# Two graph layers with layernorm: normalization on ScalarE, the adjacency scaled in its own period, two relus behind the next bank copy

## Chip, cores, metric

The kernel runs on one core of a Trainium2 chip. The metric is the device time of one execution in microseconds; a lower one is better. Runs of the kernel before agreed within 0.3% on every chip used.

## The reference, cut to what matters

There are 128 graphs of 128 nodes with 512 features, all fp32.

```python
# layer 0
deg = sum(adj, -1);  agg = (adj @ x) / max(deg, 1e-6)
x = layernorm(x + relu(concat(x, agg) @ W.T))
# layer 1
h = relu(adj @ (x @ W1) + b1)
h = relu(adj @ (h @ W2) + b2)
x = layernorm(x + adj @ (h @ W3) + b3)
# layernorm(v) = (v - mean) / sqrt(var + 1e-5), over the 512 features
```

## The kernel before

Four graphs make a period, and there are 32 periods. A period runs layer 0 and the start of layer 1 for its own graphs (`y`, `l`, `g`, `h1`) mixed with the rest of layer 1 for the graphs of the period before (`s2`, `h2`, `s3`, `o`), so that TensorE always has something to do. Each large product is made of seven smaller ones on 2x2 blocks. Three banks of PSUM (`py`, `pz`, `px`) hold them; a bank is copied to SBUF by ScalarE in the middle of the work, and **TensorE may add to that bank again only when the copy is done** (in the kernel before, the second y_y group waits for y_s in 30 periods, 108.2 us in all).

```python
def wino_a(key, a, b, c00, c11, transposed=False, inner=None):
    py, pz, px = bank(f"{key}_y"), bank(f"{key}_z"), bank(f"{key}_x")
    product(py, a, b, 1, True, transposed)
    s1 = copied(py, f"{key}_s1")            # ScalarE
    product(pz, a, b, 5, True, transposed)
    product(py, a, b, 6, False, transposed) # adds to py: waits for s1
    s2 = copied(py, f"{key}_s2")
    product(px, a, b, 2, True, transposed)
    ...
    product(py, a, b, 7, False, transposed) # waits for s2
```

The blocks that go with it (GpSimd, four instructions) are made by `data_blocks`; only those of the input x are pinned, which keeps an instruction behind all that was written before it on its engine. What isn't pinned is ordered at build time by the framework's scheduler, which may let an instruction overtake another that it takes to be not ready yet. The engines then keep that order: in the kernel before, a y_s copy whose data are there at 1025.4 starts at 1030.01, behind two relus.

```python
def data_blocks(t, name, pin=False):
    a00, a01 = t[:, 0:2, 0:2, :], t[:, 2:4, 0:2, :]
    a10, a11 = t[:, 0:2, 2:4, :], t[:, 2:4, 2:4, :]
    ...
    for dst, a, b, op in ((s1, a10, a11, OP.add), (s2, s1, a00, OP.subtract),
                          (a10, a00, a10, OP.subtract), (s4, a01, s2, OP.subtract)):
        ins = add(dst, a, b, op, nc.gpsimd)
        if pin:
            pinned(ins)

def layernorm(t, gs, name, store=None):
    ...                                     # VectorE: statistics; GpSimd: rstd
    for i, g in enumerate(gs):
        nc.vector.tensor_scalar(
            t[:, g, :], t[:, g, :], mv[:, i, 0:1], rstd[:, 1, i : i + 1], op0=OP.subtract, op1=OP.mult)

def sums_cols(q, m, n):                     # h1: add on VectorE, then relu on ScalarE
    def f(s, p):
        add(cols(H1[q], m, n), ...)
        ...
        if (m, n) == (0, 1):                # the last add
            relu_cols(q, 2, 0, 2)
            relu_cols(q, 3, 0, 2)
    return f

for t in range(NG + 1):
    ...
    if new: seg_h1_a(t)
    if old: seg_last(t - 1, (2, 3))         # o: add, layernorm, store
    if more:
        XA[t + 1] = data_blocks(XT[t + 1], f"x_{t + 1}", pin=True)
        normalized(t + 1)                   # ah = at * r on VectorE
    if new: seg_h1_b(t)                     # last add and relus of h1; then the h blocks on GpSimd
```

## Time and profile before

| | before |
|---|---|
| time, median | 2587.95 us (2587.63 to 2588.99) |
| TensorE busy | 2443.3 us, 94% |
| VectorE, ScalarE, GpSimd busy | 38%, 23%, 36% |
| longest wait of TensorE | y_y for ScalarE's copy y_s: 108.2 us in 30 times |
| mean granted clock of TensorE | 0.975 |

A row of the waits reads: who waited, for whom, us in total, times, longest. A line of the timeline reads: start, duration, engine, source line, operation, output <- input, count, and in brackets the idle time before it and what ended it. Many instructions have the line of a helper (L77 is every add), so they are told apart by their tiles: `u` and `o` are the rows that the layernorm of layer 0 and of layer 1 works on, `rstd` is 1 / sqrt(var + eps), `ah` the scaled adjacency. A name with _s is ScalarE's copy of a bank (`y_s` of `y_y`) or, on a POOL (GpSimd) line, a block sum for a product (`x_s`, `h_s`). A product has four matmuls in the program and eight in the profile. A product's group on TensorE is listed with 1.89 us, and the next one starts 1.73 us after it (in the kernel before, y_y at 1023.49 and y_z at 1025.22); for the pace one subtracts starts. The granted clock is TensorE's clock as the profiler recorded it, 1 being full speed.

### The profile page before, as it was taken

The numbers are of one execution on the slowest core, as the hardware profiler recorded it, in microseconds if no ns is written. First come the engines' busy times: TensorE is split into PE (matmuls) and PEld (weight loads), VectorE is DVE, ScalarE is ACT, GpSimd is POOL, SyncE is SP. The second block draws the span as 40 slices with busy tenths as digits, with TensorE's granted clock in tenths as the row PEclk, the third lists the DMA queues.
The fourth block names the chain that finished last, engine by engine and source line by source line (L and its number), as shares of the span: only waits on it lengthen the run. The fifth ranks groups of instructions, "written<-read, shape, count | busy, mean of one in ns | idle before, by whom it ended". The sixth has DMA issues, their size and how long they took to land.

```text
span 2585.6 us, 29247 instructions
## 1 busy us (share of the span) xinstructions
PE 2443.3 (94%) x11776; PEld 2110.4 (82%) x11776; DVE 988.5 (38%) x1685; ACT 594.9 (23%) x1025; POOL 942.9 (36%) x900
## 2 busy tenths in 40 slices
PE   6999999999999999999999999999999999999997
PEld 5888888888888888888888888888888888888886
DVE  4334433334433344333443333443334433344333
ACT  1222222222222222222222222222222222222221
POOL 1343423334333343233442343423334333344233
PEclk8999999999999999999999999999999999999999
DMA  4111101111101111011110111111112111111100
GB/s 171 46 45 62 62 29 50 46 61 62 48 32 60 46 61 62 29 49 45 62 62 29 49 45 62 62 36 42 62 45 62 57 33 49 46 62 61 29 9 33
DMA packets 53125, 133.28 MB, mean 52 GB/s; under 512 B 21632, under 2 KB 21632, under 8 KB 44800
## 3 DMA queue, kind: packets, MB, share of 16 engines
q1 hardware_dynamic: 52992, 131.42, 15.2%
q8 instruction: 94, 1.54, 0.3%
q14 instruction: 39, 0.32, 0.1%
HBM read 97.78 MB, written 33.62 MB: 51 GB/s over the span
## 4 chain that ended last, share of the span: by engine, by line
PE 81%; DVE 9%; issue 4%; ACT 3%; POOL 2%; DMA 1%; SPq 0%; POOLq 0%; DVEq 0%; ACTq 0%
PE s_y L187 17%; PE s_z L187 9%; PE l_y L187 8%; PE y_y L187 8%; PE g L304 5%; PE h L357 4%; PE s_x L187 4%; PE h_y L187 4%; PE y_x L187 2%; PE h_z L187 2%; PE y_z L187 2%; PE l_v L187 2%; PE h_x L187 2%; PE l_x L187 2%; PE l_z L187 2%
## 5 line engine op out<-in xcount | busy, mean ns | idle before, releaser
L77 POOL TENSOR_TENSOR h_s<-h 128x512 f32<-128x512 f32 x64 | 81.1, 1267 | 873.3 <-ACT h L358 837.6
L176 ACT COPY s_s<-s_y 128x512 f32<-128x512 f32 x192 | 112.4, 585 | 627.3 <-PE s_y L187 538.4
L187 PE MATMUL s_z<-w,h_s 128*128 128x256 f32 x1024 | 242.9, 380 | 2.9 <-POOL h_s L77 2.9
L187 PE MATMUL s_y<-w_t,h 128*128 128x256 f32 x1024 | 242.1, 379 | 0.7 <-ACT s_s L176 0.7
L187 PEld LDWEIGHTS s_z<-w,h_s 128*128 128x128 f32 x1024 | 194.8, 190 | 30.2 <-POOL h_s L77 3.7
L187 PEld LDWEIGHTS s_y<-w_t,h 128*128 128x128 f32 x1024 | 192.0, 190 | 25.8 <-ACT s_s L176 1.1
L187 PE MATMUL y_y<-wb_t,x_s 128*128 128x256 f32 x256 | 96.3, 542 | 108.2 <-ACT y_s L176 108.2
L77 DVE TENSOR_TENSOR s<-s_z,s_s 128x512 f32<-128x512 f32 x128 | 88.5, 692 | 258.6 <-PE s_z L187 183.4
L254 POOL TENSOR_SCALAR rstd<-mv 128x2 f32<-128x2 f32 x128 | 27.9, 218 | 437.2 <-DVE mv L252 437.2
L187 PEld LDWEIGHTS y_y<-wb_t,x_s 128*128 128x128 f32 x256 | 68.1, 278 | 132.5 <-issue 119.3
L257 DVE TENSOR_SCALAR o<-o,mv,rstd 128x512 f32<-128x512 f32 x128 | 120.8, 984 | 127.8 <-POOL rstd L255 127.8
L77 POOL TENSOR_TENSOR u<-u,b 128x512 f32<-128x512 f32 x128 | 158.2, 1267 | 0.0
L77 POOL TENSOR_TENSOR g_s<-g 128x512 f32<-128x512 f32 x32 | 40.6, 1270 | 298.3 <-ACT g L305 298.3
L304 PEld LDWEIGHTS g<-at,u 128*128 128x128 f32 x1024 | 126.7, 195 | 8.8 <-DVE u L257 5.7
L304 PE MATMUL g<-at,u 128*128 128x128 f32 x1024 | 127.1, 278 | 5.3 <-DVE u L257 5.3
L315 ACT ACTIVATE h<-h,b 128x512 f32<-128x512 f32 (+1 forms) x128 | 71.7, 607 | 246.8 <-DVE h L77 246.8
L176 ACT COPY l_s<-l_y 128x512 f32<-128x512 f32 x96 | 56.2, 585 | 310.0 <-PE l_y L187 310.0
L187 PE MATMUL l_y<-wa_t,xT 128*128 128x256 f32 x512 | 122.5, 383 | 0.0
L187 PE MATMUL s_y<-w_t,h_s 128*128 128x256 f32 x512 | 121.8, 381 | 0.0
L187 PE MATMUL h_z<-g_s,w 128*128 128x256 f32 x512 | 121.0, 379 | 0.3 <-POOL g_s L77 0.3
L187 PE MATMUL y_z<-wb,x_s 128*128 128x256 f32 x512 | 121.2, 380 | 0.0
L357 PEld LDWEIGHTS h<-at,s 128*128 128x128 f32 x1024 | 119.6, 192 | 1.8
(97 smaller groups left out, 4716.5 us busy)
## 6 DMA issues: line engine op xcount, KB each, us to landing
xT<-in_xT_dram SPq DMA_DIRECT2D x32, 1024.0 KB, 6.2
x<-in_x_dram SPq DMA_DIRECT2D x32, 1024.0 KB, 4.8
out_dram<-o SPq DMA_DIRECT2D x64, 512.0 KB, 3.0
ar<-in_adj_dram SPq DMA_DIRECT2D x32, 256.0 KB, 6.4
at<-in_adjT_dram SPq DMA_DIRECT2D x32, 256.0 KB, 6.2
r<-dd SPq DMA_DIRECT2D x32, 256.0 KB, 4.7
w<-in_w_dram SPq DMA_DIRECT2D x3, 1024.0 KB, 12.3
wb<-in_w0T_dram SPq DMA_DIRECT2D x1, 1024.0 KB, 5.6
```

What stands on the lines that cost most here:

```text
L77: return (engine or nc.vector).tensor_tensor(dst, a, b, op=op)
L176: nc.scalar.copy(t, p)
L187: nc.tensor.matmul(p[:, o, :], lhsT, rhs, start=start and o == 0 and c == 0, stop=c == 1, skip_group_check=True)
L254: nc.gpsimd.tensor_scalar(rstd[:, 0, :], mv[:, :, 1], LN_EPS, None, op0=OP.add)
L257: nc.vector.tensor_scalar(t[:, g, :], t[:, g, :], mv[:, i, 0:1], rstd[:, 1, i : i + 1], op0=OP.subtract, op1=OP.mult)
L304: nc.tensor.matmul(p[:, c, :], U[q][:, g, c * P : (c + 1) * P], AT[q][:, g, :], start=True, stop=True)
L315: nc.scalar.activation(t, t, AF.Relu, bias=b1_sb[:, c : c + 1])
L357: nc.tensor.matmul(p[:, g, :], S2[q][:, g, o * P : (o + 1) * P], AT[q][:, g, :], start=True, stop=True)
```

## The change

Its intent: the chain of VectorE work in front of the y_s copy is to become shorter (normalization goes to the idler ScalarE, the scaling of the adjacency to a quiet place), and the copy is no longer to stand behind relus that wait for that chain.

```diff
     def normalized(q):
-        AH[q] = loads.tile([P, G, P], F32, tag="ah", name=f"ah_{q}")
+        AH[q] = loads.tile([P, G, P], F32, tag="ah", name=f"ah_{q}", bufs=1)
 ...
-    normalized(0)
     w1_sb = weight_blocks(w1_raw, "w1")
 ...
-    def wino_a(key, a, b, c00, c11, transposed=False, inner=None):
+    def wino_a(key, a, b, c00, c11, transposed=False, inner=None, after_s1=None):
 ...
         s1 = copied(py, f"{key}_s1")
+        if after_s1 is not None:
+            after_s1()
 ... layernorm
-        rstd = small.tile([P, 2, k], F32, tag="rstd", name=f"rstd_{name}")
+        rstd = small.tile([P, 3, k], F32, tag="rstd", name=f"rstd_{name}")
         nc.gpsimd.tensor_scalar(rstd[:, 0, :], mv[:, :, 1], LN_EPS, None, op0=OP.add)
         nc.gpsimd.tensor_tensor(rstd[:, 1, :], rstd[:, 0, :], neg_half[:, 0:k], op=OP.pow)
+        nc.gpsimd.tensor_scalar(rstd[:, 0, :], mv[:, :, 0], -1.0, None, op0=OP.mult)
+        nc.gpsimd.tensor_tensor(rstd[:, 2, :], rstd[:, 0, :], rstd[:, 1, :], op=OP.mult)
         for i, g in enumerate(gs):
-            nc.vector.tensor_scalar(
-                t[:, g, :], t[:, g, :], mv[:, i, 0:1], rstd[:, 1, i : i + 1], op0=OP.subtract, op1=OP.mult
+            nc.scalar.activation(
+                t[:, g, :], t[:, g, :], AF.Identity, bias=rstd[:, 2, i : i + 1], scale=rstd[:, 1, i : i + 1]
             )
 ... seg_y_a
-        wino_a(f"y_{q}", XA[q], wb_sb, sums_to(Y[q], 0, 0), sums_to(Y[q], 1, 1))
+        wino_a(
+            f"y_{q}", XA[q], wb_sb, sums_to(Y[q], 0, 0), sums_to(Y[q], 1, 1),
+            after_s1=(lambda: finish_h1(q - 1)) if q >= 1 else None,
+        )
 ... sums_cols
-            if (m, n) == (0, 1):
-                relu_cols(q, 2, 0, 2)
-                relu_cols(q, 3, 0, 2)
+            if (m, n) == (1, 1):
+                relu_cols(q, 2, 1, 2)
+                relu_cols(q, 3, 1, 2)
 ... seg_h1_b
+    def finish_h1(q):
+        pinned(relu_cols(q, 2, 0, 1))
+        pinned(relu_cols(q, 3, 0, 1))
         HA[q] = data_blocks(H1[q], f"h1_{q}")
 ... the loop
         if new:
             seg_y_a(t)
+        else:
+            finish_h1(t - 1)
 ...
             seg_y_b(t)
+            normalized(t)
 ...
             XA[t + 1] = data_blocks(XT[t + 1], f"x_{t + 1}", pin=True)
-            normalized(t + 1)
```

Below, part 1 is the normalization, part 2 the adjacency scaling, part 3 the relus.

More of the change, by code (lines that the diff above doesn't have):

```diff
@@ L314, in relu_cols @@
         t = H1[q][:, c, 2 * m0 : 2 * m1, :]
-        nc.scalar.activation(t, t, AF.Relu, bias=b1_sb[:, c : c + 1])
+        return nc.scalar.activation(t, t, AF.Relu, bias=b1_sb[:, c : c + 1])
     def sums_cols(q, m, n):
```

## The prediction

> **What bounds the kernel now.** I read the page's engine shares first: TensorE computes for 94% of the span, no other engine for 40%.
>
> ```profile
> PE 2443.3 (94%) x11776; PEld 2110.4 (82%) x11776; DVE 988.5 (38%) x1685; ACT 594.9 (23%) x1025; POOL 942.9 (36%) x900
> ```
>
> So time can only come from TensorE's idle or slow moments. The waits of TensorE name them; one row dwarfs the rest:
>
> ```profile
> PE y_y L187 <- ACT y_s L176: 108.2, 30, 3.6
> PE y_y L187 <- DMA xT<-in_xT_dram: 8.9, 1, 8.9
> PE g L304 <- DVE u L257: 5.3, 1, 5.3
> PE l_x L195 <- DVE ah L146: 5.2, 1, 5.2
> ```
>
> Thirty times, once in nearly every one of 32 periods (a period handles four graphs), TensorE waits 3.6 us for ScalarE's copy y_s of the first bank of the product y. The timeline around one such wait (start us, us, engine, what) shows why a 0.56 us copy comes so late:
>
> ```profile
> 1022.82 0.71 POOL L255 TENSOR_TENSOR rstd<-rstd,neg_half 128x2 f32<-128x2 f32 x1
> ...
> 1023.49 1.89 PE L187 MATMUL y_y<-wb,xT 128*128 128x256 f32 x8
> 1023.50 1.26 POOL L77 TENSOR_TENSOR x_s<-xT 128x512 f32<-128x512 f32 x1
> 1023.57 2.89 DVE L257 TENSOR_SCALAR o<-o,mv,rstd 128x512 f32<-128x512 f32 x2 [1.14 <-POOL rstd L255]
> ...
> 1025.22 1.89 PE L187 MATMUL y_z<-wb,x_s 128*128 128x256 f32 x8
> ...
> 1026.38 1.75 DVE L146 TENSOR_TENSOR ah<-at,r 128x512 f32<-128x512 f32 x1
> ...
> 1028.05 0.68 DVE L77 TENSOR_TENSOR h<-h_z,h_s 128x512 f32<-128x512 f32 x1
> ...
> 1028.77 1.33 ACT L315 ACTIVATE h<-h,b 128x512 f32<-128x512 f32 x2 [5.96 <-DVE h L77]
> 1030.01 0.56 ACT L176 COPY y_s<-y_y 128x512 f32<-128x512 f32 x1
> ...
> 1030.71 3.38 PE L187 MATMUL y_y<-wb_t,x_s 128*128 128x256 f32 x8 [3.61 <-ACT y_s L176]
> 1033.93 1.89 PE L187 MATMUL y_x<-wb,xT 128*128 128x256 f32 x8
> ```
>
> The copy's data are there at about 1025.4, when the first y_y group ends. But on ScalarE it stands behind two relus of h; these need an add on VectorE; that add (its product h_z was done near 1023.65) stands behind two layernorm normalizations of o and the adjacency scaling ah. All of it runs while GpSimd makes the four x_s blocks.
>
> The size of the loss: the second y_y would have begun at 1025.22 + 1.73 = 1026.95 and began at 1030.71: 3.76. It then took 1033.93 - 1030.71 = 3.22 from start to start where eight such matmuls take 1.73: 1.49 more. Together 5.25 us. Check by period: one of the first g groups starts at 1000.94, the same one at 1080.67, so a period is 79.73. Its work back to back is 35 product groups of 1.727, four aggregates of 0.863, h 3.57, g 2 x 1.78 and o 2 x 1.72: 74.5. The difference, 5.2, is this one gap. Times 30: **157 us, 6.1% of the time**. Without it the kernel would take about 2588 - 157 = 2431 us.
>
> [...] 3.76 us idle, then a group at 3.22 for 1.73. Removing the gap also removes the slow group. [...] y_s is ready at 1025.4 and starts at 1030.01. So the order of the instructions on ScalarE decides this change. [...] the two o normalizations take 2.89 here (u's two take 1.01 with GpSimd idle), and ah 1.75 here where in the first period, alone, it took 0.69. [...] The trace has the form with bias alone at 0.71 (L315, 128x512)[...]. [...]
>
> **The change part by part.**
> *Normalization to ScalarE.* Removes from VectorE, per period, four u normalizations (0.54 each) and four o (0.98 mean): 6.1 us. [...] ScalarE's busy time rises from 595 to some 790, 32%: no bound. GpSimd gets two more small instructions per pair (-mean, times rstd). By L254 (0.22) and a gap of 0.08 each that is 0.6 us per pair, 2.4 per period, and it lies **on the path**: each normalization comes 0.6 later.
> *Adjacency scaling.* ah moves to about 1050, behind the last y add, where VectorE is idle for over 2 us. It is needed at 1059.8, and r is there since the period before. It costs nothing there and frees VectorE here. One buffer is enough: its last reader is the aggregate at about 1071.
> *Relus.* Two of the four half-relus (0.45 each) move up behind the add at 1019.14; the other two move behind y_s. So y_s waits no longer for the last h add.
>
> At the old gap, then: h add at about 1023.7 to 1024.4; rstd ready about 1024.15; two o normalizations on ScalarE to about 1025.65; y_s to 1026.25; the second y_y at 1026.95 **without a wait**, 0.7 to spare. The relus follow to 1027.2, GpSimd finishes x_s by about 1029.6 (four at 1.27 to 1.4), the h blocks by 1034.7; the first is needed at about 1033.9 and is ready at 1030.9. The gap goes whole: -157.
>
> New waits[...]:
> (a) The x_s blocks stand behind the 0.6 us of new GpSimd work: the first ends at 1025.4 instead of 1024.76, and y_z's weights are loaded from 1025.0. Wait 0.3 to 0.4.
> (b) In u's layernorm the first rstd is ready at about 1077.5, where the second s_s copy is ready at 1077.4 and the next s_y wants it done by 1078.94. Behind two normalizations it ends at 1079.6 (wait 0.7), behind four at 1081.3 (wait 2.4, unless the scheduler has put the g matmuls first, then 0.6), before them none. Mean by my weights 1.0.
> (c) In o's first layernorm rstd is ready about 1015.6 (GpSimd does the g blocks until 1013.9), and the second h_s copy is ready at 1015.07. If normalizations are ahead of it, it ends at 1017.7 and h_y7, due 1016.59, waits 1.1. I take 0.4 as the mean.
> Sum 1.75 per period, 30 x 1.75 = 53 us. First period and tail: a later last normalization (+1), a tail wait for h_s (2.55) that shortens by about 1: nothing. 2588 - 157 + 53 = 2484; since the scheduler fills holes that it sees with other ready matmuls I lean a little lower: **2474 us**.
>
> **Rivals.** *The wait only changes place:* ScalarE, in order, holds bank copies behind normalizations that wait for GpSimd. For it: the eight new instructions fall among the copies, and rstd took 1.14 us where a scheduler may reckon less. Against it: normalizations are ready within a microsecond or two of the copies, and none sits behind a 6 us chain. If (b) and (c) are at their worst, 2.4 and 1.1 with a dropped clock after one (+1.5): 5.2 per period, and the time stays at 2580. *GpSimd becomes the bound:* 36% busy, +2.4 of 80 us per period: no, but it is the engine of (a). *The gap was hidden anyway:* no; the chain of waits goes through it and the period's sum shows it bare. *All gone, nothing new:* 2431.
>
> **Range and chances.** The floor is 2431; the middle has 1 to 2.5 us of new waits per period (2460 to 2506); a bad order of ScalarE gives 2530 and more. So 2433 to 2534. Faster by over 2% needs under 2536, that is new waits under 3.5 us per period: 0.89. Within 2% 0.10, slower 0.01.
>
> **What would show it.** Right: the row of y_y waiting for y_s is gone; the slow y_y group is back at 1.73; o normalizations no longer appear on VectorE, ah takes 0.69; a period lasts 74.8 to 77; small new rows name y_z waiting for x_s, s_y for s_s, h_y for h_s. Wrong: one of these rows with over 3 us each time, with a slow group behind it.

## The result, and the profile after

| | before | after |
|---|---|---|
| time, median of 4 | 2588.01 us | 2592.41 us |
| VectorE busy | 988.5 us | 779.0 us |
| ScalarE busy | 594.9 us | 792.8 us |
| mean granted clock of TensorE | 0.975 | 0.996 |
| y_y waiting for y_s | 108.2 us | no such row |

The ratio is 1.0016, with a 95% interval of 0.9999 to 1.0034: the time is the same. Ratios here are the mean time of one kernel's fast runs over that of the other's fast runs of the same rounds, so they are not quite the ratio of the medians quoted. The predicted 2474 us, and the range up to 2534, were wrong.

The busy line of the changed kernel's page:

```profile
PE 2423.8 (94%) x11776; PEld 2077.1 (80%) x11776; DVE 779.0 (30%) x1429; ACT 792.8 (31%) x1345; POOL 974.2 (38%) x1156
```

The work moved as planned, and TensorE is as far from full as before. Its waits in the changed kernel:

```profile
PE s_y L186 <- ACT s_s L175: 55.4, 33, 1.7
PE y_z L186 <- POOL x_s L77: 34.0, 30, 1.3
PE h_y L186 <- ACT h_s L175: 31.5, 31, 1.0
PE y_y L186 <- POOL x_s L77: 13.8, 30, 0.5
```

The old wait has gone, and four new rows stand in its place, each once per period: 4.3 us per period by these rows. The timeline of one period shows how each is made; the first five lines belong to s_y, the next three to h_y, the rest to y_z and y_y:

```profile
998.96 1.52 ACT L260 ACTIVATE u<-u,rstd 128x512 f32<-128x512 f32 x2 [2.90 <-POOL rstd L258]
...
1000.45 0.61 PE L310 MATMUL g<-at,u 128*128 128x128 f32 x4
1000.66 1.52 ACT L260 ACTIVATE u<-u,rstd 128x512 f32<-128x512 f32 x2 [0.18 <-POOL rstd L258]
...
1002.09 0.56 ACT L175 COPY s_s<-s_y 128x512 f32<-128x512 f32 x1
1002.79 1.96 PE L186 MATMUL s_y<-w_t,h 128*128 128x256 f32 x8 [1.73 <-ACT s_s L175]
...
1018.84 1.52 ACT L260 ACTIVATE o<-o,rstd 128x512 f32<-128x512 f32 x2 [3.38 <-POOL rstd L258]
...
1020.27 0.56 ACT L175 COPY h_s<-h_y 128x512 f32<-128x512 f32 x1
...
1020.97 1.97 PE L186 MATMUL h_y<-g,w_t 128*128 128x256 f32 x8 [1.01 <-ACT h_s L175]
...
1028.27 1.27 POOL L77 TENSOR_TENSOR h_s<-h 128x512 f32<-128x512 f32 x1
1029.49 0.20 POOL L258 TENSOR_TENSOR rstd<-rstd 128x2 f32<-128x2 f32 x1
1029.64 1.26 POOL L77 TENSOR_TENSOR x_s<-xT 128x512 f32<-128x512 f32 x1
...
1030.86 1.27 POOL L77 TENSOR_TENSOR h_s<-h_s,h 128x512 f32<-128x512 f32 x1
1030.96 1.99 PE L186 MATMUL y_z<-wb,x_s 128*128 128x256 f32 x8 [1.12 <-POOL x_s L77]
1031.15 0.56 ACT L175 COPY y_s<-y_y 128x512 f32<-128x512 f32 x1
...
1032.10 1.26 POOL L77 TENSOR_TENSOR x_s<-x_s,xT 128x512 f32<-128x512 f32 x1
...
1033.41 1.99 PE L186 MATMUL y_y<-wb_t,x_s 128*128 128x256 f32 x8 [0.46 <-POOL x_s L77]
1035.24 1.89 PE L186 MATMUL y_x<-wb,xT 128*128 128x256 f32 x8
```

- **s_y**: the second s_s copy stands behind all four normalizations of u, which end at 1002.2; its data are there at about 998.9 (the group before it starts at 997.00 and is listed with 1.89), and it starts at 1002.09. The scheduler filled part of the hole with four g matmuls (0.44 us). TensorE is idle from 1000.90 to 1002.79, and the group after it takes 0.07 more than 1.73: 1.96 us in all.
- **h_y**: the second h_s copy stands behind the first two normalizations of o. Idle 1.17 us, and the restart 0.07: 1.24.
- **y_z and y_y**: on GpSimd, one of the four h blocks stands ahead of the last small instruction of rstd, and so ahead of the first x_s block; a second one stands between the first and second x_s block. The first x_s block starts at 1029.64, though its input xT was there before: TensorE reads it from 1027.94 on. By starts: y_z begins 1.29 late, y_y follows 0.72 late, and the group after y_y 0.10: 2.11.

The sum is 1.96 + 1.24 + 2.11 = 5.3 us per period, against the 5.25 that the old gap had cost. That the two are so close is a coincidence of sizes: no run links them, and each new wait can be removed alone (below). A period is 79.80 us (s_x at 998.73, the next at 1078.53), where it was 79.73.

### The profile page after: what moved, and what is told of

Its sections match the earlier page's. It is cut to its first block, busy times and chain, and to the rows that moved or that the text cites. A ratio compares the mean times of both kernels' runs of the same rounds, so it can differ in the third digit from the quotient of the medians.

```text
span 2590.0 us, 29418 instructions
## 1 busy us (share of the span) xinstructions
PE 2423.8 (94%) x11776; PEld 2077.1 (80%) x11776; DVE 779.0 (30%) x1429; ACT 792.8 (31%) x1345; POOL 974.2 (38%) x1156
## 4 chain that ended last, share of the span: by engine, by line
PE 63%; POOL 19%; DVE 7%; ACT 6%; issue 4%; DMA 1%; SPq 0%; POOLq 0%; ACTq 0%; DVEq 0%
PE s_y L186 13%; PE l_y L186 8%; PE y_y L186 7%; PE s_z L186 6%; POOL g_s L77 5%; PE h L367 4%; PE g L310 4%; POOL rstd L256 4%; DVE st L252 3%; POOL h_s L77 3%; POOL x_s L77 3%; PE h_y L186 3%; PE s_x L186 2%; PE y_z L186 2%; PE l_v L186 2%
## 5 line engine op out<-in xcount | busy, mean ns | idle before, releaser
L186 PE MATMUL s_y<-w_t,h 128*128 128x256 f32 x1024 | 244.4, 382 | 54.3 <-ACT s_s L175 54.3
L255 POOL TENSOR_SCALAR rstd<-mv 128x2 f32<-128x2 f32 x128 | 28.1, 219 | 416.5 <-DVE mv L253 411.1
L260 ACT ACTIVATE o<-o,rstd 128x512 f32<-128x512 f32 x128 | 97.2, 806 | 190.4 <-POOL rstd L258 190.4
L186 PE MATMUL h_y<-g,w_t 128*128 128x256 f32 x512 | 123.4, 384 | 31.5 <-ACT h_s L175 31.5
L186 PEld LDWEIGHTS h_y<-g,w_t 128*128 128x128 f32 x512 | 94.7, 190 | 68.1 <-issue 57.9
L186 PEld LDWEIGHTS y_z<-wb,x_s 128*128 128x128 f32 x512 | 95.5, 191 | 58.1 <-POOL x_s L77 46.1
L260 ACT ACTIVATE u<-u,rstd 128x512 f32<-128x512 f32 x128 | 97.2, 806 | 106.5 <-POOL rstd L258 106.5
L77 DVE TENSOR_TENSOR s<-s_x,s_s 128x512 f32<-128x512 f32 x64 | 44.3, 692 | 276.9 <-PE s_x L186 276.9
```

The source lines that it names most:

```text
L77: return (engine or nc.vector).tensor_tensor(dst, a, b, op=op)
L186: nc.tensor.matmul(p[:, o, :], lhsT, rhs, start=start and o == 0 and c == 0, stop=c == 1, skip_group_check=True)
L255: nc.gpsimd.tensor_scalar(rstd[:, 0, :], mv[:, :, 1], LN_EPS, None, op0=OP.add)
L260: nc.scalar.activation(t[:, g, :], t[:, g, :], AF.Identity, bias=rstd[:, 2, i : i + 1], scale=rstd[:, 1, i : i + 1])
```

## The experiments

The theory, called ORDER: the gain was made and given back, by three groups of instructions that each stand too early in an in-order queue. Its main rival, LENGTH: the chain to the normalized rows has become too long (two more instructions on GpSimd, 0.8 us instead of 0.54 for u), and another order would only move the wait. A third question is which of the three parts made the gain.

### Keeping the h blocks behind the x_s blocks

```diff
-        HA[q] = data_blocks(H1[q], f"h1_{q}")
+        HA[q] = data_blocks(H1[q], f"h1_{q}", hold=True)   # hold: pinned, as for x
```

> The changed kernel with one thing undone: the four h blocks on GpSimd are kept behind the four x_s blocks. Theory ORDER (the lost gain is three waits, each made by one instruction that stands too early in an in-order queue): y_z's wait for x_s falls from 1.13 us to about 0.3 (only the two small new GpSimd instructions are left of it), y_y's wait of 0.46 goes; of the 2.1 us per period lost there 1.8 comes back, 30 times, 54 us: 2538 us. The waits for s_s and h_s stay at 1.7 and 1.0. Rival LENGTH (the chain to rstd is simply too long, four GpSimd instructions and ScalarE's 0.8 us per normalization, wherever things stand): x_s stays late, 2575 or more.

Measured: 2535.39 us, ratio 0.9798 (0.9782 to 0.9814). The wait of y_z for x_s is left once (0.3 us) and that of y_y for x_s has gone; the rows of s_s and h_s are as they were (54.3 and 31.4 us). That is 57 us below the changed kernel, where ORDER said 54 and LENGTH at most 17.

### Normalizing behind the bank copies

All instructions are the same and on the same engines. Only the place of these normalizations on ScalarE differs (and with the first o, that of the store behind it; the first period's u and the last period's o are left as they were).

```diff
         s2 = copied(py, f"{key}_s2")
+        if after_s2 is not None:
+            after_s2()          # s3: the four normalizations of u; h1: the first two of o
 ... layernorm, for these
+        late.append(norm)       # called in after_s2, each instruction pinned
```

> The changed kernel with the same instructions, but on ScalarE the u normalizations stand behind the second s_s copy and the first pair of o behind the second h_s copy. GpSimd unchanged. ORDER: the waits of s_y for s_s (1.73 us, 1.97 with its restart) and of h_y for h_s (1.01, 1.24) go, 31 times 3.2 = 99 us: 2493 us; y_z for x_s stays near 1.1. LENGTH: the wait only goes to g for u and to later h copies; 2560 or more.

Measured: 2492.39 us, ratio 0.9631 (0.9616 to 0.9645). The rows of h_s and, but for 1.7 us in two times, of s_s have gone; those of x_s stay (34.1 and 13.9 us). 100 us came back, and g did not begin to wait for u in the periods that followed the first.

### Both orders mended

> Both orders mended, all three parts of the change and the whole longer chain kept. ORDER: 2592 - 54 - 99 = 2439 us, TensorE's waits under 0.5 us per period. LENGTH: 2530 or more.

Measured: 2435.66 us, ratio 0.9412 (0.9398 to 0.9426). The first waits of TensorE that are left:

```profile
PE y_y L186 <- DMA xT<-in_xT_dram: 8.9, 1, 8.9
PE g L328 <- ACT u L263: 6.1, 1, 6.1
PE l_x L194 <- DVE ah L146: 5.3, 1, 5.3
```

These three occur once, at the start. The gains add up: 57 + 100 = 157 us, and together 2592.41 - 2435.66 = 156.8. All of the longer chain is still in this kernel, so LENGTH is refuted as the cause of the loss; what the chain may still cost here is the 8 us by which this kernel stands above part 3 alone (below).

### u on VectorE again, and the first o on VectorE again

Two checks of the single waits from the other side: the instructions that stood ahead of a copy leave ScalarE.

```diff
-            layernorm(U[q], (2 * m, 2 * m + 1), f"0_{q}_{m}")
+            layernorm(U[q], (2 * m, 2 * m + 1), f"0_{q}_{m}", on_act=False)   # first kernel
-        layernorm(o, (0, 1), f"1_{q}_{gs[0]}")
+        layernorm(o, (0, 1), f"1_{q}_{gs[0]}", on_act=gs[0] == 2)             # second kernel
```

> The changed kernel with u's normalization back on VectorE (o stays on ScalarE). Both theories: the wait of s_y for s_s goes, 31 x 1.97 = 61 us: 2531 us, the other two waits stay. If something other than the place of u's normalizations on ScalarE holds s_s back, the row stays and the time with it.

Measured: 2527.26 us, ratio 0.9767 (0.9752 to 0.9781). The row of s_s falls from 55.4 to 1.7 us; h_s keeps 27.9, x_s 34.0 and 13.8.

> The changed kernel with only the first pair of o normalized on VectorE again. ORDER: the wait of h_y for h_s (1.01 us, 1.24 with its restart) goes and nothing else: 2592 - 31 x 1.24 = 2554 us. If h_s is late for another reason, its row stays.

Measured: 2555.26 us, ratio 0.9874 (0.9859 to 0.9888). The row of h_s has gone and the others stayed: 37 us below the changed kernel, 38 expected. With these two each wait has its size: s_y 65 us, h_y 37, the x_s waits 57.

### Part 1 alone

> The kernel before with part 1 alone: normalization on ScalarE; the relus and the adjacency scaling stay where they were. Theory ORDER: s_s waits (1.97 us per period with restart) and h_s waits (1.24) appear as in the changed kernel; y_z waits for x_s at most 0.3, as no h block is ready ahead of x_s; the y_y gap shrinks to about 0.7, since the two relus and y_s stand behind the o normalizations (end near 1025.7) on ScalarE. Loss 3.9 to 4.3 of the former 5.25: 2588 - 30 x 1.1 = 2555, range 2540 to 2570. Rival NORM IS THE BOON (taking normalization off VectorE is what cures the gap): under 2520.

Measured: 2559.79 us, ratio 0.9896 (0.9882 to 0.9911). The waits for s_s (53.9 us) and h_s (31.1) are there, and y_z waits for x_s (11.7 us in 30 times), while the h blocks come behind all four x_s blocks here. y_y has no row for y_s, so the 0.7 expected there did not show as a wait of its own; in the period that I read, y_y starts 0.39 us late (1019.99, after y_z at 1017.87). It starts just behind the y_s copy, which stands behind the two relus and ends at 1019.85: the old wait, shrunk to 0.4. The normalization on ScalarE by itself, with its own early orders unmended, is thus worth 1%.

### Part 2 alone

> The kernel before with part 2 alone: the adjacency scaling moved to its own period. The last h add comes 1.67 us earlier, so the gap of 3.76 becomes 2.1. If the clock still drops after 2.1 us idle: 30 x 1.67 = 50 us, 2538. If it doesn't: 30 x 3.1 = 94, 2494. Rival (the chain is set by something else than ah): no change, 2588.

Measured: 2528.69 us, ratio 0.9776 (0.9761 to 0.9790). The timeline of TensorE at the gap:

```profile
1002.53 1.89 PE L186 MATMUL y_z<-wb,x_s 128*128 128x256 f32 x8
1006.36 3.20 PE L186 MATMUL y_y<-wb_t,x_s 128*128 128x256 f32 x8 [1.94 <-ACT y_s L175]
1009.36 2.38 PE L186 MATMUL y_x<-wb,xT 128*128 128x256 f32 x8
1011.58 1.89 PE L186 MATMUL y_y<-wb_t,xT 128*128 128x256 f32 x8
```

The gap shrank as computed, from 3.76 to 1006.36 - 1002.53 - 1.73 = 2.10 us, and it does so in each of the 30 periods. In this one the clock still dropped: the two products after the gap took 3.00 and 2.22 us from start to start, where 1.73 is usual. In others it did not, after the same gap:

```profile
1397.98 1.97 PE L186 MATMUL y_y<-wb_t,x_s 128*128 128x256 f32 x8 [1.93 <-ACT y_s L175]
1399.79 1.89 PE L186 MATMUL y_x<-wb,xT 128*128 128x256 f32 x8
```

Counted over the whole trace (mean granted clock 0.982), the clock halved at 20 of the 30 gaps (1.76 us lost behind each, on the mean) and stayed whole at 10 (0.07 lost). The kernel before is no different: of its 30 gaps of 3.77 us, 21 halved the clock (11 lost 1.5 us, 10 lost 2.7) and 9 did not (the product from 1110.43 took 1.81). So what was lost behind the gaps is 44 us in the kernel before and 36 here; with 30 x 1.67 = 50 us of shorter gaps that makes 58, and 58 was measured. The expectation had only "always" (50) and "never" (94).

### Part 3 alone, with the h blocks kept behind

Normalization is on VectorE and the adjacency scaled in its old place. (The scratch tile of rstd keeps its unused third row.)

```diff
-            if (m, n) == (0, 1):
-                relu_cols(q, 2, 0, 2)
-                relu_cols(q, 3, 0, 2)
+            if (m, n) == (1, 1):
+                relu_cols(q, 2, 1, 2)
+                relu_cols(q, 3, 1, 2)
 ... finish_h1 behind the y_s copy, as in the change
+        HA[q] = data_blocks(H1[q], f"h1_{q}", hold=True)
```

> The kernel before with part 3 alone, h blocks kept behind x_s: normalization and adjacency stay on VectorE where they were[...]. ORDER: y_s no longer stands behind the relus, so the whole gap goes though the VectorE chain is as long as ever: 2588 - 157 = 2431, up to 2440. Rival (the VectorE chain is the bound, and would only turn up at the next reader of h or of the freed bank): over 2500.

Measured: 2427.68 us, ratio 0.9384 (0.9369 to 0.9400). The timeline at the place of the old gap:

```profile
1039.99 2.89 DVE L260 TENSOR_SCALAR o<-o,mv,rstd 128x512 f32<-128x512 f32 x2 [1.14 <-POOL rstd L257]
...
1041.63 1.89 PE L187 MATMUL y_z<-wb,x_s 128*128 128x256 f32 x8
1041.89 0.59 ACT L176 COPY y_s<-y_y 128x512 f32<-128x512 f32 x1 [2.67 <-PE y_y L187]
...
1042.80 1.75 DVE L146 TENSOR_TENSOR ah<-at,r 128x512 f32<-128x512 f32 x1
...
1043.36 1.89 PE L187 MATMUL y_y<-wb_t,x_s 128*128 128x256 f32 x8
...
1044.47 0.68 DVE L77 TENSOR_TENSOR h<-h_z,h_s 128x512 f32<-128x512 f32 x1
```

The whole VectorE chain is there as before: 2.89 us for the two normalizations, 1.75 for ah, the last h add at 1044.47. But y_s starts when its data are there, y_y follows y_z after 1.73, and nobody needs the late add soon. This is the fastest kernel together with the next one, and it contains only one part of the change, and the hold, which the change does not have.

### Parts 2 and 3, and part 3 without the hold

> Parts 2 and 3 with the normalization left on VectorE, h blocks kept behind x_s. ORDER: nothing is left to gain over part 3 alone: 2431 to 2438. If VectorE's chain still matters, 10 us or more below part 3 alone.

Measured: 2427.35 us, ratio 0.9385 (0.9371 to 0.9399): the same as part 3 alone. The adjacency scaling is worth 58 us while the gap is there and nothing once it is not.

> Part 3 alone as the change has it, the h blocks free on GpSimd. Built, the first h block stands between the first and the second x_s block. ORDER: the second x_s block ends one block (1.27 us) later, at about 1027.5 where y_y wants it at 1026.95; wait 0.5 to 0.7 per period, 30 x 0.65 = 20 us over part 3 with the h blocks kept behind: 2448 us (2440 to 2460). Rival (the h block disturbs only together with the longer chain of part 1): 2428.

Measured: 2452.08 us, ratio 0.9477 (0.9461 to 0.9493). One row is new:

```profile
PE y_y L187 <- POOL x_s L77: 16.2, 30, 0.7
```

So the early h block is a side effect of part 3, and costs 24 us with the short chain already (the two runs are from two chips; the ratios, 0.9477 and 0.9384, differ by as much). Why it can come early: the first block adds a10 and a11 of h. In the kernel before, the relu of a11 came together with that of a01, behind the last add. Part 3 relus a11 earlier, and leaves only a01 for later, which only the fourth block reads. With part 1 alone, where the relus stay, the h blocks come behind all x_s blocks. That the scheduler took the first blocks for ready and GpSimd for idle there is the likely reason; no run shows its reckoning.

## Why the prediction was wrong, point by point

- **The bound and its size were right.** The gap of y_y was put at 157 us, the time without it at 2431; part 3 alone gave 2427.7. There was luck in the size: it was 30 times the one gap that was read, which lost 1.49 us to the clock, where the thirty lost 0.07, 1.5 or 2.7; their mean happens to be 1.48.
- **The clock step was right in sum.** The slow groups after the gap disappeared, and the mean clock rose from 0.975 to 0.996. But "3.76 us idle, then a slow group" is not a rule of this trace: in 9 of 30 periods the same gap left the clock whole.
- **The costs of the moved work were right.** ScalarE's busy time was put at some 790 us, the author's estimate, and was 792.8, with 0.806 us for a normalization; the two new GpSimd instructions took 0.23 and 0.20, with their gaps the 0.6 predicted; ah took 0.68.
- **"Second y_y without a wait" was right for y_s**, whose row is gone. What it now waits for is x_s.
- **The step that failed is the sum of new waits, 1.75 us per period, which was 5.3.** Terms (b) and (c) had the right mechanism and too small a weight; (a) lacked its main cause:
  - (a) was put at 0.3 to 0.4 and was 2.11. The term counted only the two small instructions ahead of x_s. Mended in order, that is what they cost: y_z 0.20 late and its own group 0.10 longer, 30 x 0.30 = 9 us; 2435.66 - 2427.68 gives 8 us, across two chips and with intervals that just overlap. The rest came from the h blocks. The prediction took them to follow x_s ("finishes x_s by about 1029.6, the h blocks by 1034.7") and did not ask what each h block reads, although part 3 changes just that.
  - (b) was put at 1.0 and was 1.96. Of the four orders listed the one with all four normalizations ahead of s_s came, with a few g matmuls pulled forward: 1.89 us of idle time and 0.44 of g matmuls make 2.33, near the 2.4 that had been listed for it.
  - (c) was put at 0.4 and was 1.24. Again the order that had been listed with 1.1 came.
- **"I lean a little lower" leaned the wrong way.** The scheduler filled 0.44 us of one hole. The normalizations were written earlier in the program than the copies, and they had the earlier place in both spots. A mean over orders was taken where the program's order was known.
- **The rival "the wait only changes place" came true**: its worst case said 5.2 us per period and 2580 us (its terms, 2.4, 1.1 and 1.5, add up to 5.0, which is what 2580 goes with). It hit the time by luck: it had a dropped clock in its sum, which did not happen, and left (a) out. The prediction gave all outcomes within 2% or slower 0.11 together.
- **One thing was not asked: whether all three parts are needed.** The y_s copy stood behind relus that waited for the long chain. Moving the relus is enough, if the h blocks are kept behind x_s; the chain may then be as long as it was.

## What to carry to other kernels

When a copy is late because it stands behind something in an in-order queue, first take it out from behind that, before making what it waited for faster: here the first gave 159 us (136 without the hold on the h blocks), and making the chain shorter as well gave nothing more (part 2) or cost time (part 1). Work moved to another engine lands in that engine's queue, so ask for every place in the period which short, urgent instruction it will stand ahead of, and pin it behind that. And when an instruction's inputs become ready earlier, look at what it may now overtake.

## What else the traces show

- The length of the gap did not decide whether the clock dropped: 2.10 us (part 2 alone) halved the clock in 20 of 30 periods, 3.77 us (the kernel before) left it whole in 9 of 30. In the clock records of the kernel before, each halved stretch lasts 3.41 or 6.83 us (the one at the end of the run apart) and begins on one fixed grid of 3.41 us steps. Counting TensorE's idle time (from the starts of its matmuls) step by step in that trace, each of the 25 full-clock steps that were idle for 0.64 of their length or more (2.2 us) was followed by a halved one, and none that was idle for 0.61 or less. The nine gaps of 3.77 us that left the clock whole are each cut in two by a step's border and fill at most 0.61 of a step. The 1.89 us before s_y in the changed kernel fill at most 0.56 of a step, and no drop follows.
- Very small instructions on GpSimd differ: for 128x2 elements the changed kernel's trace shows 0.22 us for an add with a constant (L255), 0.20 for a multiplication of two tiles (L258), but 0.71 for a power (L256); the power is over half of the four instructions of rstd.
- A restart after a short wait at full clock has a small cost: the first product group took 1.80 us instead of 1.73 after 1.17 us of idle time and after 1.89 (the changed kernel), and 1.80 to 1.81 after those gaps of 2.10 (part 2 alone) and 3.77 (the kernel before) that left the clock whole.
